# A state-space block between two feed-forward parts: the output projection of 29 phases in seven products of quarters

## The chip, the cores and the metric

The kernel runs on one core of a Trainium2 chip. The metric is the time of one execution in device microseconds, as the median of several runs. TensorE multiplies matrices into PSUM, VectorE (DVE) and ScalarE (ACT) work on PSUM and SBUF, GpSimd (POOL) on SBUF, and SyncE (SP) issues the transfers. Each engine takes its instructions in order.

## The reference

The input is 2 sequences of 512 tokens with 512 features, all in float32. The network adds four parts to it one after the other, each behind a layer norm: a block-sparse linear layer, a gated feed-forward part with quantised weights (512 to 1792 to 512), a state-space part with 128 heads of 64, and the same feed-forward part again. The state-space part, which the change is about, is this:

```python
proj = hidden_states @ in_proj_w.T                 # gate (8192), x (8192), B and C (8 groups of 128 each), dt
hBC = silu(causal_conv4(x, B, C))                  # four taps along the tokens
dt = softplus(dt + dt_bias)
Y_diag = einsum(M, x*dt)                           # inside chunks of 128 tokens
Y_off  = einsum(C, states) * state_decay           # from the chunks before
y = Y_diag + Y_off + D*x
y = y * rsqrt(mean(y*y) + EPS) * norm_w
y = y * silu(gate)
return y @ out_proj_w.T                            # 8192 -> 512
```

## The kernel before

The inner width 8192 is cut into 64 tiles of 128 features. A phase handles two tiles (`PP = 2`); there are 32 phases. A unit is one tile of one sequence, so a phase has four units (j, b). The loop over phases is a pipeline: in phase `ph` the front makes the x and gate projections of tiles 2ph and 2ph+1, the back runs the scan of phase ph-1, and the output projection is that of phase ph-2.

The x and gate projections already use seven products of quarters instead of eight (`seven`, L169): the weights' and the normed input's quarters are combined by additions (`left_sides` on GpSimd, `two_quarters` and others on the input), and seven products of two 128x128 by 128x512 matmuls each go into three PSUM accumulators. VectorE and ScalarE take partial sums out of them between the products. `seven` is a generator: each `next` puts one product with its additions into the queues.

The rest of a phase:

- `x_tokens` (L798): four transposes of a unit on TensorE, the multiply by dt on VectorE (`x_dt`), the decay on GpSimd (`x_dec`).
- `states` (L820): three matmuls into `pst`, then on VectorE one copy (L833) and four steps of 128x64 (L836).
- `scores` (L857): on ScalarE four activations, an exponential of `m` and one of `ce`; on VectorE, when `flush` is called, the multiply `m*gm` (L874); on GpSimd the multiply of `ce` (L880).
- `scan` (L888): the matmuls of a unit into one PSUM bank `py`; afterwards `gated` (L910) on VectorE takes it out (L912) and multiplies the gate into it in place (L913). The result, `gts[j, b]`, is 128 features by 512 tokens.
- `conv` (L706): ScalarE starts the convolution (L708), three further taps on VectorE (L711) are queued and put out by `drain`.
- `squares` (L918): a square on ScalarE and a sum on GpSimd (L920).
- `out_project` (L922): for each of the eight tiles of 128 tokens two matmuls 128x128 by 128x512 into one PSUM bank `po`, and one addition on VectorE into `acc` (L939). `acc` is the tile `x_sb`, 128 x 8 x 512.

PSUM has eight banks: three with the tag `proj`, three with `yo`, two with `tr`. In the phases from 2 on, the eight output products stand behind the first two scans, with `flush`, the scores and two to three taps between them, and the last two scans and the gate product follow:

```python
for k in range(4):
    between(2 * k)          # outs(2k)
    flush()
    if last or k:
        back_scores(4 + k)
    if last:
        drain(1 if k < 3 else 0)
```

The order of TensorE, VectorE and ScalarE is that of the program (`tc.manual_schedule`). GpSimd's and SP's queues are ordered by a planner. Every fourth phase also makes the B and C projections of the next group of eight tiles (`new_group`), seven products more.

Of the kernel before, what the change touches and what calls it, by code (L numbers as in the profile page):

```python
# [14 lines left out]
P = 128  # L15
# [22 lines left out]
def kernel(  # L38
# [42 lines left out]
    def weights():  # L81
        return keep.tile([P, KC, 2, P], F32, tag="w", name="w", bufs=3)
# [75 lines left out]
    def left_sides(w):  # L158

        a11, a12, a21, a22 = w[:, :KH, 0], w[:, KH:, 0], w[:, :KH, 1], w[:, KH:, 1]  # L160
        sq = keep.tile([P, 3, KH, P], F32, tag="ws", name="ws", bufs=3)
        s1, s2, s4 = sq[:, 0], sq[:, 1], sq[:, 2]
        nc.gpsimd.tensor_add(s1, a21, a22)  # L163
        nc.gpsimd.tensor_sub(a21, a11, a21)
        nc.gpsimd.tensor_sub(s2, s1, a11)
        nc.gpsimd.tensor_sub(s4, a12, s2)
        return a11, a12, a21, a22, s1, s2, s4

    def seven(left, tag, tmp, done, in_place):  # L169
# [16 lines left out]
        x, y, z = [psum.tile([P, SEQ], F32, tag=tag, name=f"{tag}{i}", bufs=3) for i in range(3)]  # L186
# [3 lines left out]
        yield  # L190
        product(y, s2, t2, True, False)
# [43 lines left out]
    def dequant_in(s, w, z, sc, scratch):  # L235

        cols = slice(s * SLAB, (s + 1) * SLAB)
        q = weights()
# [30 lines left out]
    def dequant_gate(s, scratch):  # L269
        return dequant_in(s, gate_w, gate_z, gate_s, scratch)  # L270

    def dequant_up(s, scratch):
        return dequant_in(s, up_w, up_z, up_s, scratch)
# [109 lines left out]
    def ffn(which, first, waiting, after, within):  # L383
# [3 lines left out]
        with tc.tile_pool(name=f"ffn{which}", bufs=1) as pool:  # L387
# [19 lines left out]
            def sg_tile(j, b):  # L407
                return pool.tile([P, SEQ], F32, tag=f"sg{j}{b}", name="sg")

# [44 lines left out]
            for b in range(2):  # L454
# [20 lines left out]
                if b == 0:  # L475
                    gq_next = left_sides(now(dequant_gate(1, scratch)))
                    quarters()
            last_quarter()
            uq_next = left_sides(now(dequant_up(1, scratch)))
            dequant_down(0)  # L480
            gq, uq = gq_next, uq_next
            for s in range(1, NSLAB):
# [18 lines left out]
                if more:  # L501
                    gq = left_sides(now(dequant_gate(s + 1, scratch)))
# [7 lines left out]
                if more:  # L510
                    uq = left_sides(now(dequant_up(s + 1, scratch)))
# [65 lines left out]
    def load_pair(*cts):  # L577

        w = weights()
# [11 lines left out]
        return left_sides(w)  # L591
# [9 lines left out]
    def step_weights():  # L601
        w_dt = weights()[:, :, 0, :]
# [43 lines left out]
    def mixer(waiting, step_args, loaded):  # L646

        with ExitStack() as st:
# [93 lines left out]
            def group_scores(made, shared, bs=range(2)):  # L742
                for b in bs:
                    b_t, c_t = made[b]
                    b_tok = grp.tile([P, NCH - 1, P], F32, tag=f"b_tok{b}", name="b_tok")
# [26 lines left out]
            def load_sums(ct, b):  # L772

                h0 = 2 * ct
                bc = wrk.tile([P, 2, SEQ], F32, name="bc", bufs=3)
# [12 lines left out]
            def g_front(left, gts):  # L788

                for j, b in units:  # L790
# [3 lines left out]
                    left, "proj", lambda j, b: gts[j, b], lambda j, b, ps: later.append((gts[j, b], ps)), False  # L794
# [25 lines left out]
            def states(ct, b, x_dec, b_tok):  # L820
# [12 lines left out]
                nc.vector.tensor_copy(state[:, 0], pst[:, 0])  # L833
# [54 lines left out]
            def scan(ct, b, xc, gt, x_dt, state, heads, tag):  # L888

                py = psum.tile([P, SEQ], F32, tag=tag, name="py", bufs=3)  # L890
# [54 lines left out]

            xcs, gts = {}, {}
# [14 lines left out]
            wg = load_pair(0, 1)  # L961
# [80 lines left out]
            for ph in range(1, n_ph + 1):  # L1042
# [39 lines left out]
                if last:  # L1082
                    wo = load_out(ph - 2)
                if not front:
# [4 lines left out]
                final = ph == n_ph - 1  # L1089
                if final:  # L1090
# [10 lines left out]
                next(steps)  # L1101
                if not last:
                    group_scores(made, groups[0], [0])
                else:
                    flush()
                next(steps)
                if not last:
                    group_scores(made, groups[0], [1])
                    made = None
                    flush()  # L1110
                else:
                    back_scores(2)
                tokens(2)
                tokens(3)
                next(steps)
                if last:
                    back_scores(3)
                next(steps)
                flush()
                if not last:  # L1120
                    back_scores(4)
                both_states(0)
                next(steps)
                drain(3)
                next(steps)
                run(steps)
                if not last:
                    drain(3)
                if last:
                    both_states(1)  # L1130
                scans = half_scan(units[:2])
                if not last:
                    drain()
                    both_states(1)
                    gate, later = g_front(wg, gts_new)
                else:
                    finish(scans)
                    scans = []

                def between(k):  # L1140
                    if last:
                        outs(k)
                    else:
                        next(gate, None)

                for k in range(4):
                    between(2 * k)
                    flush()
                    if last or k:
                        back_scores(4 + k)  # L1150
                    if last:
                        drain(1 if k < 3 else 0)
                    if made and k in (1, 2):
                        group_scores(made, groups[c0 // CTG], [k - 1])
                    between(2 * k + 1)
                    if k == 0:
                        finish(scans[:1])
                    elif k == 1:
                        finish(scans[1:])
                        scans.clear()  # L1160
                    if last:
                        drain(1 if k < 3 else 0)
                flush()
                all_squares()
                drain()
                made = None
                if new_group:


                    steps, made = group((c0 + PP) // CTG, wbc, "yo")  # L1170
                    for i, _ in enumerate(steps):
                        if i in (3, 5):
                            drain(3)
                if ph + 1 < n_ph:
                    wx = load_pair(NCT + c0 + PP, NCT + c0 + PP + 1)
                if last:
                    gate, later = g_front(wg, gts_new)
                if final:
                    up_q = weights()
                    ups = [dequant_half(up_q, 0, 0, up_w, up_z, up_s, old_tmp)]  # L1180
                finish(half_scan(units[2:], "proj" if new_group else "yo"))
                if last:
                    next(gate)
                else:
                    for u in units:
                        silu(xcs_new[u], xcs_new[u])
                half_scores(0, c0, heads_new)
                if last:
                    next(gate)
                if final:  # L1190
                    for f in gates:
                        f()
                    ups.append(dequant_half(up_q, 1, 0, up_w, up_z, up_s, old_group))
                drain(3)
                half_scores(1, c0, heads_new)
                if last:
                    next(gate)
# [225 lines left out]
```

## Time and profile before

| | us |
|---|---|
| median of 3 runs | 2285.58 (2284.93 to 2286.6) |
| the profiled execution | 2286.75 |
| its span | 2285.0 |
| TensorE busy | 2266.0 (99%) |
| VectorE busy | 1669.7 (73%) |
| ScalarE busy | 1162.5 (51%) |
| GpSimd busy | 1014.9 (44%) |
| output projection, L927, 992 matmul records | 436.8 |
| its additions, L939, 248 | 167.9 |

The busy time of an engine is that of its instructions in the profiled execution; matmul records overlap, so their sum is more than the time they occupy. The granted clock of TensorE was 0.999. A plain phase takes 49.0 us, one with a new group 61.0 and the one behind it 51.45.

### The profile page before, as it was taken

The numbers are of one execution on the slowest core, as the hardware profiler recorded it, in microseconds if no ns is written. First come the engines' busy times: TensorE is split into PE (matmuls) and PEld (weight loads), VectorE is DVE, ScalarE is ACT, GpSimd is POOL, SyncE is SP. The second block draws the span as 40 slices with busy tenths as digits, with TensorE's granted clock in tenths as the row PEclk, the third lists the DMA queues.
The fourth block names the chain that finished last, engine by engine and source line by source line (L and its number), as shares of the span: only waits on it lengthen the run. The fifth ranks groups of instructions, "written<-read, shape, count | busy, mean of one in ns | idle before, by whom it ended". The sixth has DMA issues, their size and how long they took to land.

```text
span 2285.0 us, 28307 instructions
## 1 busy us (share of the span) xinstructions
PE 2266.0 (99%) x10008; PEld 1273.9 (56%) x10008; DVE 1669.7 (73%) x2926; ACT 1162.5 (51%) x2474; POOL 1014.9 (44%) x971
## 2 busy tenths in 40 slices
PE   9999999999999999999999999999999999999999
PEld 5445865555555555555555555555555555544468
DVE  5456568787788787877877887888878778865553
ACT  4111056756665665666566556656565665631100
POOL 3765024545544444444445444444444454526620
PEclk9999999999999999999999999999999999999999
DMA  5663022222222222222122222221222321326600
GB/s 190 190 201 107 24 82 71 74 71 68 75 74 74 66 82 74 65 74 83 65 74 74 75 70 69 79 78 56 84 74 65 106 71 65 111 84 230 205 16 28
DMA packets 145773, 201.46 MB, mean 88 GB/s; under 512 B 7136, under 2 KB 92000, under 8 KB 145632
## 3 DMA queue, kind: packets, MB, share of 16 engines
q1 hardware_dynamic: 145056, 198.61, 27.0%
q8 instruction: 79, 1.29, 0.2%
q10 hardware_dynamic: 576, 1.05, 0.1%
q14 instruction: 62, 0.51, 0.1%
HBM read 194.91 MB, written 4.72 MB: 87 GB/s over the span
## 4 chain that ended last, share of the span: by engine, by line
PE 96%; DVE 2%; ACT 1%; DMA 1%; issue 0%; POOL 0%; ACTq 0%; SPq 0%; POOLq 0%; DVEq 0%
PE proj L177 39%; PE po L927 19%; PE yo L177 10%; PE ffn_o L533 7%; PE py L893 5%; PE pst L825 4%; PE py L902 3%; PE x_tr L804 2%; PE pg L463 1%; PE pu L463 1%; PE bs_o L323 1%; PE pgm L755 1%; PE ln_tr L134 0%; DMA bias_b<-in_bias_dram 0%; DVE xc L711 0%
## 5 line engine op out<-in xcount | busy, mean ns | idle before, releaser
L880 POOL TENSOR_TENSOR ce<-ce,c_t 128x384 f32<-128x384 f32 x256 | 267.4, 1049 | 450.9 <-ACT ce L876 445.1
L927 PE MATMUL po<-wo,gt 128*128 128x512 f32 x992 | 436.8, 595 | 0.0
L177 PE MATMUL proj<-xn_t,w 128*128 128x512 f32 x912 | 424.8, 596 | 3.3 <-DVE gt L192 1.7
L866 ACT ACTIVATE m<-bc,acs 128x128 f32<-128x128 f32 x1024 | 324.5, 389 | 4.4 <-PE py L893 4.4
L927 PEld LDWEIGHTS po<-wo,gt 128*128 128x128 f32 x992 | 184.6, 190 | 219.6 <-issue 194.4
L177 PE MATMUL proj<-tq,ws 128*128 128x512 f32 x608 | 278.5, 592 | 1.3 <-ACT gt L726 1.3
L177 PEld LDWEIGHTS proj<-xn_t,w 128*128 128x128 f32 x912 | 165.6, 190 | 182.6 <-issue 170.2
L874 DVE TENSOR_TENSOR m<-m,gm 128x512 f32<-128x512 f32 x256 | 219.2, 876 | 0.4 <-ACT m L873 0.4
L163 POOL TENSOR_TENSOR ws<-w 128x256 f32<-128x256 f32 x96 | 72.2, 752 | 323.3 <-DMA w<-in_win_t_dram 319.7
L711 DVE SCALAR_TENSOR_TENSOR xc<-proj,cw,xc 128x511 f32<-128x511 f32 (+2 forms) x288 | 213.3, 741 | 2.5
L812 POOL TENSOR_TENSOR x_dec<-x_dt,dec 128x384 f32<-128x384 f32 x128 | 131.6, 1038 | 130.8 <-DVE x_dt L808 122.3
L177 PEld LDWEIGHTS proj<-tq,ws 128*128 128x128 f32 x608 | 112.9, 190 | 131.2 <-issue 123.2
L920 POOL TENSOR_TENSOR sq_acc<-sq_acc,y 128x512 f32<-128x512 f32 x128 | 175.4, 1384 | 19.3 <-ACT y L919 19.2
L939 DVE TENSOR_TENSOR x_sb<-x_sb,po 128x512 f32<-128x512 f32 x248 | 167.9, 677 | 21.9 <-PE po L927 20.5
L893 PE MATMUL py<-m,x_dt 128*64 128x128 f32 x2048 | 180.9, 276 | 0.1
L873 ACT ACTIVATE m<-m 128x512 f32<-128x512 f32 x256 | 161.3, 630 | 7.4
L708 ACT ACTIVATE xc<-proj,cb,cw 128x512 f32<-128x512 f32 x96 | 71.2, 775 | 164.3 <-DVE proj L206 146.3
L902 PE MATMUL py<-ce,state 128*64 128x128 f32 x1536 | 149.5, 273 | 0.0
L177 PE MATMUL proj<-xn_t,ws 128*128 128x512 f32 x304 | 142.8, 592 | 0.0
L177 PE MATMUL proj<-tq,w 128*128 128x512 f32 x304 | 142.8, 592 | 0.0
L893 PEld LDWEIGHTS py<-m,x_dt 128*64 128x64 f32 x2048 | 122.1, 137 | 29.7 <-issue 20.5
L189 ACT COPY gt<-proj 128x512 f32<-128x512 f32 x32 | 18.7, 585 | 228.6 <-PE proj L177 228.5
(202 smaller groups left out, 3707.1 us busy)
## 6 DMA issues: line engine op xcount, KB each, us to landing
bc<-acs_d SPq DMA_DIRECT2D x128, 512.0 KB, 3.7
w<-in_win_t_dram SPq DMA_DIRECT2D x64, 512.0 KB, 3.8
wo<-in_wo_t_dram SPq DMA_DIRECT2D x31, 512.0 KB, 3.3
wi<-in_down_w_dram SPq DMA_DIRECT2D x14, 512.0 KB, 3.5
zi<-in_down_z_dram SPq DMA_DIRECT2D x14, 512.0 KB, 4.4
sf<-in_down_s_dram SPq DMA_DIRECT2D x14, 512.0 KB, 3.9
wi<-in_gate_w_dram SPq DMA_DIRECT2D x13, 512.0 KB, 4.1
zi<-in_gate_z_dram SPq DMA_DIRECT2D x13, 512.0 KB, 5.2
```

Of the source, the lines that this page charges most:

```text
L177: nc.tensor.matmul(ps, lhsT=a[:, kc, :], rhs=b[:, kc, :], start=(start and kc == 0), stop=(stop and kc == KH - 1), skip_group_check=True,)
L533: nc.tensor.matmul(ps, lhsT=a[:, k, :], rhs=b(k), start=(start and k == 0), stop=(stop and k == KF - 1), skip_group_check=True,)
L711: nc.vector.scalar_tensor_tensor(dst[:, s:], ps[:, : SEQ - s], cw[:, t, 3 - s : 4 - s], dst[:, s:], ALU.mult, ALU.add)
L866: nc.scalar.activation(m[:, c, :], bc[:, hh, c * P : (c + 1) * P], AF.Relu, bias=acs[:, t, h : h + 1], scale=-1.0,)
L873: nc.scalar.activation(m, m, AF.Exp, scale=-1.0)
L874: mults.append(lambda: nc.vector.tensor_mul(m, m, shared[b][2]))
L880: nc.gpsimd.tensor_mul(ce, ce, c_t[:, P:].rearrange("p (c l) -> p c l", l=P))
L893: nc.tensor.matmul(py[hh * HD : (hh + 1) * HD, c * P : (c + 1) * P], lhsT=x_dt[:, c, hh, :], rhs=m[:, c, :], start=True, stop=(c == 0),)
L902: nc.tensor.matmul(py[hh * HD : (hh + 1) * HD, c * P : (c + 1) * P], lhsT=state[:, c - 1, hh, :], rhs=ce[:, c - 1, :], start=False, stop=True,
L920: nc.gpsimd.tensor_add(sq_acc[:, b, :], sq_acc[:, b, :], y)
L927: nc.tensor.matmul(po, lhsT=gts[j, b][:, c * P : (c + 1) * P], rhs=wo[:, j, :], start=(j == 0), stop=(j == PP - 1),)
L939: nc.vector.tensor_add(acc[:, t, :], acc[:, t, :], po)
```

## The change

For the output projection of phases 0 to 28 (29 of 32) a phase's product, 1024 tokens by 256 features by 512 outputs, is cut into quarters: two sequences, two feature tiles, two halves of 256 outputs. Seven products of quarters replace eight. GpSimd makes three sums of the activations and changes one quarter in place (`out_left`), and does the same with the output weights (`out_right`).

Each product of a quarter is put out in two rounds (`r`) of two 128-token tiles: two matmuls 128x128 by 128x256 into one PSUM bank. So a phase has 14 such steps, each of two matmuls and one addition of 2x256 columns on VectorE. Three banks accumulate (x, y, z), and VectorE adds them, while they accumulate further, to the four quarters of `acc` and to a fifth accumulator, `common`, which takes the weights' third buffer. After phase 28's projection `merge` adds `common` to three quarters. The first round of seven steps stands between the steps of the x projection, the second behind the first two scans.

Other edits: the state's first copy moves from VectorE to ScalarE; the last two scans use the `tr` banks; the taps of the last two x results are put out in the gate product, or in the group's; in phases without a new group the gate product uses one `proj` and two `yo` banks; `bc` has two buffers instead of three, `b_tok` one instead of two; `w` and `ws` have two and a third under a tag of its own.

```diff
-        x, y, z = [psum.tile([P, SEQ], F32, tag=tag, name=f"{tag}{i}", bufs=3) for i in range(3)]
+        tags = [tag] * 3 if isinstance(tag, str) else tag
+        def bank(i):
+            return psum.tile([P, SEQ], F32, tag=tags[i], name=f"{tags[i]}{i}", bufs=3)
+        x = bank(0)
...
         yield
+        y, z = bank(1), bank(2)
...
-                bc = wrk.tile([P, 2, SEQ], F32, name="bc", bufs=3)
+                bc = wrk.tile([P, 2, SEQ], F32, name="bc", bufs=2)
...
-                nc.vector.tensor_copy(state[:, 0], pst[:, 0])
+                nc.scalar.copy(state[:, 0], pst[:, 0])
...
-                py = psum.tile([P, SEQ], F32, tag=tag, name="py", bufs=3)
+                py = psum.tile([P, SEQ], F32, tag=tag, name="py", bufs=2 if tag == "tr" else 3)
...
+            def out_right(wo):
+                b11, b12, b21, b22 = wo[:, 0, :DH], wo[:, 0, DH:], wo[:, 1, :DH], wo[:, 1, DH:]
+                t = sides(True).rearrange("p i k c -> p i (k c)")
+                nc.gpsimd.tensor_sub(t[:, 0], b12, b11)
+                nc.gpsimd.tensor_sub(t[:, 1], b22, t[:, 0])
+                nc.gpsimd.tensor_sub(b12, b22, b12)
+                nc.gpsimd.tensor_sub(t[:, 2], b21, t[:, 1])
+                return b11, t[:, 0], b21, b22, t[:, 1], b12, t[:, 2]
+            def out_left(gts):
+                a11, a12, a21, a22 = gts[0, 0], gts[1, 0], gts[0, 1], gts[1, 1]
+                s = sc.tile([P, 3, SEQ], F32, tag="sums", name="sums")
+                nc.gpsimd.tensor_add(s[:, 0], a21, a22)
+                nc.gpsimd.tensor_sub(a21, a11, a21)
+                nc.gpsimd.tensor_sub(s[:, 1], s[:, 0], a11)
+                nc.gpsimd.tensor_sub(s[:, 2], a12, s[:, 1])
+                return a11, a12, s[:, 0], s[:, 1], a21, s[:, 2], a22
+            def out_seven(left, right, fresh):
...
+                def product(r, k, start, stop, a, b):
+                    if start:
+                        banks[k] = psum.tile([P, 2, DH], F32, tag="yo", name="po7", bufs=3)
+                    for c in range(2):
+                        t = slice((2 * r + c) * P, (2 * r + c + 1) * P)
+                        nc.tensor.matmul(
+                            banks[k][:, c, :],
+                            lhsT=a[:, t],
+                            rhs=b,
+                            start=(start and c == 0),
+                            stop=stop,
+                            skip_group_check=True,
+                        )
+                def summed(r, k, q, new):
+                    q = q[:, 2 * r : 2 * r + 2]
+                    if fresh and new:
+                        nc.vector.tensor_copy(q, banks[k])
+                    else:
+                        nc.vector.tensor_add(q, q, banks[k])
...
+                    for k, start, stop, a, b, q, new in (
+                        ("x", True, False, a11, b11, common[0], True),
+                        ("y", True, False, s2, t2, q12, True),
+                        ("z", True, False, s1, t1, q22, True),
+                        ("x", False, True, a12, b21, q11, True),
+                        ("y", False, False, s3, t3, q22, False),
+                        ("z", False, True, s4, b22, q12, False),
+                        ("y", False, True, a22, t4, q21, True),
+                    ):
...
+            def merge():
+                for rows, cols in quarter[1:]:
+                    nc.gpsimd.tensor_add(acc[:, rows, cols], acc[:, rows, cols], common[0])
...
+                if mid:                      # phases 2 to 30
+                    outs7 = out_seven(lefts, rights, ph == 2)
+                    def o():
+                        product, summed = outs7.pop(0)
+                        product()
+                        summed()
+                    next(steps); o()
+                    next(steps); o()
+                    back_scores(2); tokens(2); tokens(3)
+                    o()
+                    next(steps); back_scores(3); o()
+                    next(steps); o()
+                    flush(); both_states(0)
+                    next(steps); back_scores(4); o()
+                    drain(3)
+                    next(steps); drain(3); o()
+                    run(steps)
+                    both_states(1)
+                    scans = half_scan(units[:2])
+                    finish(scans[:1]); o()
+                    finish(scans[1:]); o()
+                    flush(); back_scores(5); o(); o()
+                    flush(); back_scores(6)
+                    if made:
+                        group_scores(made, groups[c0 // CTG], [0])
+                    o(); o()
+                    flush(); back_scores(7)
+                    if made:
+                        group_scores(made, groups[c0 // CTG], [1])
+                    o()
+                    all_squares()
...
+                    if new_group:
+                        flush()
+                        steps, made = group((c0 + PP) // CTG, wbc, "yo")
+                        for i, _ in enumerate(steps):
+                            if i in (0, 1, 3, 5):
+                                drain(3)
+                        gate, later = g_front(wg, gts_new)
+                    else:
+                        gate, later = g_front(wg, gts_new, ("proj", "yo", "yo"))
+                        next(gate); flush()
+                    wx = load_pair(NCT + c0 + PP, NCT + c0 + PP + 1)
+                    wo = load_out(ph - 1)
+                    finish(half_scan(units[2:], "tr"))
+                    if ph < n_ph - 2:
+                        lefts, rights = out_left(gts), out_right(wo)
+                    if new_group:
+                        next(gate)
+                    half_scores(0, c0, heads_new); next(gate)
+                    drain(3)
+                    half_scores(1, c0, heads_new); next(gate)
+                    if not new_group:
+                        drain(3)
...
+                    next(gate)
+                    if new_group:
+                        drain(3)
+                    flush(); run(gate)
```

Calls that stand on lines of their own in the program are joined here with semicolons.

## The prediction

> **What bounds the kernel now.** I read the page first: engines, then the chain of waits, then the groups. TensorE is busy for all but 19 us of the span and owns the chain, so a matmul that goes away is time, as long as nothing else becomes late.
>
> ```profile
> PE 2266.0 (99%) x10008; PEld 1273.9 (56%) x10008; DVE 1669.7 (73%) x2926; ACT 1162.5 (51%) x2474; POOL 1014.9 (44%) x971
> PE 96%; DVE 2%; ACT 1%; DMA 1%; issue 0%; POOL 0%; ACTq 0%; SPq 0%; POOLq 0%; DVEq 0%
> ```
>
> Then the chain in order of time, which cuts one phase of the mixer (811.84 to 860.84, 49.0 us) into its stretches, and shows a stretch of 256-wide products in the first feed-forward part.
>
> ```profile
> 220.05 39.28 PE ffn_o L533 x182
> 811.84 12.21 PE proj L177 x28
> 824.92 3.44 PE proj L177 x8
> 829.23 3.44 PE proj L177 x8
> 834.01 5.15 PE proj L177 x12
> 843.71 13.93 PE po L927 x32
> ```
>
> A float32 matmul is two records here (L927: 992 records in 31 phases of 16 matmuls). So a 512-wide record takes 13.93 / 32 = 0.435 us in the output projection, 12.02 / 28 = 0.429 in the x and gate products, and a 256-wide one 39.28 / 182 = 0.216.
>
> Last the windows of the two halves of that phase, and VectorE's timeline in it. The columns of the windows are busy us with the count for PE, PEld, DVE, ACT, POOL.
>
> ```profile
> 811.84:836.00 24.16, 24.16 (x78) 12.34 (x79) 14.14 (x21) 19.02 (x40) 12.46 (x14) 1.00 0.21 65
> 836.00:860.84 24.84, 24.84 (x165) 14.77 (x163) 24.39 (x51) 11.88 (x29) 10.89 (x11) 1.00 0.26 87
> ```
>
> ```profile
> 832.71 0.69 DVE L197 TENSOR_TENSOR tmp<-tmp,proj 128x512 f32<-128x512 f32 x1 [2.35 <-PE proj L177]
> ```
>
> The reader should see that the share "DVE 73%" hides a stretch in which VectorE is busy for 24.39 of 24.84 us. It keeps up there only because each result of the output projection (two 512-wide matmuls, 1.74 us) asks for one addition.
>
> ```profile
> 834.03 2.09 DVE L874 TENSOR_TENSOR m<-m,gm 128x512 f32<-128x512 f32 x2
> 836.05 0.28 DVE L833 COPY state<-pst 128x128 f32<-128x128 f32 x1
> 836.36 0.86 DVE L836 SCALAR_TENSOR_TENSOR state<-state,e_last,pst 128x64 f32<-128x64 f32 x4
> 838.22 2.31 DVE L711 SCALAR_TENSOR_TENSOR xc<-tmp,cw,xc 128x511 f32<-128x511 f32 x3
> 840.46 0.69 DVE L206 TENSOR_TENSOR proj<-tmp,proj 128x512 f32<-128x512 f32 x1
> 841.05 0.69 DVE L211 TENSOR_TENSOR proj<-tmp,proj 128x512 f32<-128x512 f32 x1
> 843.84 0.74 DVE L912 SCALAR_TENSOR_TENSOR y<-xc,dsk,py 128x512 f32<-128x512 f32 x1
> 844.62 0.75 DVE L913 SCALAR_TENSOR_TENSOR gt<-y,nw,gt 128x512 f32<-128x512 f32 x1
> 846.73 0.68 DVE L939 TENSOR_TENSOR x_sb<-x_sb,po 128x512 f32<-128x512 f32 x1
> ```
>
> From start to start VectorE spends 0.60 on an addition that reads PSUM, 0.72 where the next needs its result, 2.24 on three taps, 0.77 on a unit's four state steps, 0.78 and 0.67 on L912 and L913. The multiply L874 takes 0.61 with GpSimd idle (820.27: two in 1.28) and 1.02 with it busy (834.03); its mean is 0.876.
>
> **The change, part by part.** I number the products of a changed phase X1..X7 (x), O1..O14 (output: two rounds of seven), G1..G7 (gate).
>
> TensorE. 16 matmuls, 13.93 us, become 28 of 256: 56 x 0.2158 = 12.08. Saved 1.85 a phase, 29 phases: -53.7 us. The weights load in 190 ns, below 216, as they do in L533.
>
> VectorE. The eight additions become fourteen of the same 512 elements, +3.6 us a phase; four copies (L833, 0.31 each) go to ScalarE. In sum VectorE still fits (38.5 busy of 49.0, then about 41.5 of 47.2), so the place decides. I walk its queue, as the built program orders it, from the end of X4, t = 0, where it is idle and waiting (the row at 832.71). O5 add, two L874, states, O6 add, three taps, X6 add, three taps, O7 add, X7 add: 1.32 + 0.60 + 1.22 + 1.54 + 0.60 + 2.24 + 0.60 + 2.24 + 0.60 + 0.60 = 11.56, with L874 at its 0.61. The first 1.32 are the two adds of X4. Now the moved copy: ScalarE has it behind the convolution start of X7 (L708, 0.74), which waits for VectorE's X7 add to end (0.69). A 128x128 copy on ScalarE is not in the trace; L866 of that size has 0.39. VectorE goes on 0.69 + 0.03 + 0.74 + 0.39 + 0.02 = 1.87 after it began the X7 add instead of 0.60: 1.27 idle. A copy of 0.28, as on VectorE, would make it 1.16. Then the states of two units, 1.54, and L912 of the first unit, 0.75: with 0.03 from TensorE to VectorE at the start it ends at 15.1.
>
> TensorE in the same time: O5 0.86, states 1.33, X5 1.72, O6 0.86, X6 1.72, O7 0.86, X7 1.72, states 1.33, two scans 3.22, O8 0.86 = 14.48. O9 takes the PSUM bank of the first scan, free only after that L912: it waits 0.65. O10 takes the second's bank: L913 0.67, O8 add 0.60, L912 0.75 end 2.05 after the first L912; TensorE is there at 0.96: 1.1 more. O14 accumulates on O12's result after VectorE has added it: L913, O9, L874, O10, O11, L874, O12 add end 6.4 after the first L912, TensorE is there at 5.6: 0.9 more with 0.1 for the handover. Stall 2.7 with every L874 at 0.61. Four of them lie on this path; the two of the early part stand beside GpSimd's x_dec exactly as the row at 834.03 does. At 1.02 each the stall is 4.3; I take the mean, 0.876: 3.8.
>
> What is late next: the six taps of X6 and X7 now stand in the gate stretch. After the third scan (end P): two units' L912 and L913 until P + 3.1, G2 add from P + 3.55, taps until P + 8.6, G4's first add ends at P + 9.3; G6 needs it and could start at P + 8.67: 0.7. Phases that bring a new group have seven more products between and four taps fewer there, so they lack this.
>
> The sum by kind: 15 plain phases, 3.8 + 0.7 - 1.85 = +2.66 each, +39.9. Seven with a new group, 3.8 - 1.85, +13.7. Seven behind those, where the group scores (2.44 of TensorE) cover O14's wait: 0.65 + 0.53 + 1.1 + 0.7 - 1.85 = +1.1 each, +7.9. Together +61.5. With L874 at 0.61 the three kinds give +1.55, +0.85 and +0.6, in all +33; at 1.02 +3.15, +2.45 and +1.4, in all +74.
>
> GpSimd gets four 512-wide and four 256-wide operations a phase: 4 x 1.27 (L920 alone) + 4 x 0.73 (L163) = 8.0, on 23.4 busy of 49.0. They are due at O2, 4.3 us into the next phase; the four of the activations stand behind the ce of the next heads and end about 3 us after that phase's nominal start. I cost them at nothing; each us later would be 29 us. The load of wo (3.3 us to landing) now waits for O14, stands on SP's queue ahead of one sums load (3.7) and has the 15 us of G and scans as cover. The x weights wait for X7 (4.0 from issue to their sides in this trace), then four sides (2.9) stand ahead of three ce on GpSimd; the last ends near 33.5 against the fourth scan at 35, without stalls. Two sums buffers instead of three: each load still has one whole unit's time, over 6 us. The merge is three GpSimd additions of 128x1024 once, 2.4 each by L231, behind the last round and some 30 us before its sums are read: between 0 and 7 us in all, taken as 0. The weight tags hold the same three buffers.
>
> A rule against the change is in the Trainium skill, GPSIMD Engine Reference, section Key points: GpSimd shares its SBUF interfaces with VectorE and collides with VectorE instructions that have two SBUF inputs. L874 shows it (0.61 against 1.02). L913 has two SBUF inputs as well, and shows 0.75 at 844.62 with a ce multiply of GpSimd starting inside it, and 0.75 with none. By the rule L913 would stretch like L874, and the one between L912 and O10 would add about 0.4 a phase, 12 us; I leave that out.
>
> The profiled execution took 2286.75 for a span of 2285.0, and the median of the runs is 2285.58. 2286.75 + 61.5 = 2348; less the 1.2 between execution and median, 2347. I forecast 2346.
>
> **The rivals.** (A) VectorE keeps pace and the matmuls' saving comes through. For it: VectorE's sum fits, and the first half of the phase has 10 us of idle (24.16 against 14.14) into which seven additions moved. Against it: O9, O10 and O14 hang on the second half. It decides at O12's add: the chain of 21.5 us before it must be over 2 us shorter than the rows make it, and the taps must not hold G6. In full -53.7: 2232; half, 2259. (B) The copy on ScalarE is not late, because the convolution start finds VectorE ahead: 29 x 1.27 = 37 less, 2309, or 2282 with L874 at 0.61. The row for ScalarE's order speaks against it, the unmeasured copy leaves room. (C) GpSimd becomes late as well, sums after O2 or every L874 beside it: one us a phase more, 2375.
>
> **How the numbers follow.** Forecast case (2318 to 2360 on its own) 0.56, A 0.22, B 0.13, C 0.09. About 0.2%, 4.6 us, is what a measurement of this kernel can tell from no change: B gives 0.05 of that, the rest of B is slower. Slower 0.56 + 0.08 + 0.09 = 0.73, the same 0.05, faster 0.22. The range reaches from 2268 (leaving out most of A and nothing of B, 0.16) to 2370 (leaving out the upper part of C, 0.04).
>
> **What would show it.** Right: plain phases of 51 to 52 us instead of 49.0; in TensorE's groups the output product with idle before it, released by VectorE's gating and additions, about 3 to 4 us a phase; VectorE idle for about 1.2 us before the second states, released by ScalarE. TensorE busy about 2212. Wrong: phases of 47.2, or TensorE waiting for GpSimd or a transfer.

## The result and the profile after

The changed kernel takes 2435.25 us (2431.08 to 2438.38) against 2285.99 for the kernel before in the same measurement: a ratio of 1.0652 [1.0632, 1.0672], 149.3 us slower. The profiled execution took 2438.4 for a span of 2436.7. The direction was as forecast; the forecast of 2346 and its range up to 2370 were not.

In the changed program the lines stand 23 further down: the multiply by the group scores is L897 (was L874), the gating L935 and L936 (L912, L913), the taps L734 (L711). L1014 is the new output product, L1028 its addition, L185 the x and gate products. From the page, engines and chain:

```profile
PE 2302.0 (94%) x10704; PEld 1436.7 (59%) x10704; DVE 1812.8 (74%) x2972; ACT 1192.8 (49%) x2602; POOL 1264.5 (52%) x1206
PE 62%; DVE 32%; ACT 2%; issue 2%; DMA 1%; POOL 1%; ACTq 0%; DVEq 0%; SPq 0%; POOLq 0%
```

VectorE's share of the chain went from 2% to 32%. TensorE's busy time rose, although it has less to do, and that is the first sign of something that the prediction did not have. The waits of TensorE (us in total, times, longest):

```profile
PE po L1014 <- DVE y L935: 82.7, 53, 2.8
PE yo L185 <- DVE gt L211: 19.7, 22, 1.3
PE po L1014 <- DVE x_sb L1028: 10.5, 18, 0.8
```

The places are those forecast: O9 and O10 wait for the gating (L935), O14 for an addition, G6 for the taps behind which L211 stands. TensorE's timeline of a plain phase, 816.12 to 869.35, shows O9, O10, O14 and G6:

```profile
844.93 1.94 PE L1014 MATMUL po<-ws,sums 128*128 128x256 f32 x4 [2.06 <-DVE y L935]
847.07 1.82 PE L1014 MATMUL po<-ws,sums 128*128 128x256 f32 x4 [0.19 <-DVE y L935]
851.75 1.13 PE L1014 MATMUL po<-ws,gt 128*128 128x256 f32 x4 [0.27 <-DVE x_sb L1028]
865.65 1.98 PE L185 MATMUL yo<-tq,w 128*128 128x512 f32 x4 [0.79 <-DVE gt L211]
```

O9 waits 2.06, not 0.65 to 1.18, and then O9 and O10 take 1.94 and 1.82 where four such records take 1.03 elsewhere. The windows tell why (the last columns are the granted clock, the DMA share and GB/s):

```profile
816.12:869.35 53.23, 49.92 (x266) 32.24 (x265) 44.10 (x72) 31.88 (x72) 32.01 (x32) 0.97 0.21 70
844.90:848.30 3.40, 3.17 (x7) 2.13 (x8) 3.35 (x6) 3.37 (x11) 2.48 (x2) 0.53 0.42 154
```

Right behind the gap the granted clock is half for 3.4 us. The trace's clock records hold 32 such stretches with 132.7 us in all, 28 of them in the 29 changed phases; the kernel before has 2 with 6.3 us.

VectorE's timeline in that phase is the queue that the prediction walked:

```profile
830.15 2.27 DVE L897 TENSOR_TENSOR m<-m,gm 128x512 f32<-128x512 f32 x2
834.48 3.10 DVE L734 SCALAR_TENSOR_TENSOR xc<-tmp,cw,xc 128x511 f32<-128x511 f32 x3
838.09 2.31 DVE L734 SCALAR_TENSOR_TENSOR xc<-proj,cw,xc 128x511 f32<-128x511 f32 x3
842.60 1.62 DVE L859 SCALAR_TENSOR_TENSOR state<-state,e_last,pst 128x64 f32<-128x64 f32 x8 [1.00 <-ACT state L856]
844.14 0.74 DVE L935 SCALAR_TENSOR_TENSOR y<-xc,dsk,py 128x512 f32<-128x512 f32 x1
```

and GpSimd beside it:

```profile
829.80 2.07 POOL L835 TENSOR_TENSOR x_dec<-x_dt,dec 128x384 f32<-128x384 f32 x2 [3.53 <-PE pst L848]
835.24 0.99 POOL L903 TENSOR_TENSOR ce<-ce,c_t 128x384 f32<-128x384 f32 x1 [3.37 <-ACT ce L899]
```

L935 ends 16.7 us after the end of X4 instead of 15.1. From start to start two rows make the difference: the pair of L897 took 2.19 (1.22 at the short price, 1.75 at the mean that was taken), and the first three taps 3.01 instead of 2.24. Both have GpSimd beside them. The three taps behind have it too, and took 2.22, the time of taps without it:

```profile
838.61 0.73 POOL L171 TENSOR_TENSOR ws<-w 128x256 f32<-128x256 f32 x1 [2.37 <-PE pst L848]
```

The difference is in the inputs: the first three read `tmp` and `xc`, both in SBUF, the three behind read `proj`, which is in PSUM, and `xc`. Over the whole trace, a tap of `tmp` took at most 0.75 with GpSimd idle (65 of them) and 1.10 to 1.54 where a GpSimd instruction ran when it started (27); none of the 288 taps of `proj` took over 0.75, though GpSimd ran at the start of 208. The copy on ScalarE left VectorE idle for 1.00, forecast 1.27.

By kind, from the start of a phase to the next (the phases before: plain 49.0, with a new group 61.0, behind a group 51.5, the first 42.3, the second 52.2):

| kernel | median us | ratio [95%] | plain | new group | behind a group | stretches at half clock |
|---|---|---|---|---|---|---|
| after | 2435.25 | 1.0652 [1.0632, 1.0672] | 54.4 | 65.3 | 56.5 | 32 |
| e1 gate product between | 2379.41 | 1.0406 [1.0390, 1.0421] | 52.7 | 63.3 | 53.9 | 2 |
| e2 multiplies early | 2359.79 | 1.0321 [1.0305, 1.0336] | 51.9 | 62.9 | 53.0 | 2 |
| e3 no additions | 2275.05 | 0.9951 [0.9937, 0.9965] | 48.4 | 59.4 | 51.0 | 3 |
| e4 no sums | 2425.88 | 1.0608 [1.0592, 1.0624] | 54.1 | 65.8 | 55.0 | 25 |
| e5 copy on VectorE | 2441.04 | 1.0660 [1.0639, 1.0682] | 54.7 | 65.6 | 57.4 | 30 |
| e6 three together | 2302.70 | 1.0069 [1.0054, 1.0085] | 49.7 | 60.5 | 52.0 | 2 |
| e7 taps first | 2312.02 | 1.0106 [1.0090, 1.0122] | 50.4 | 60.4 | 52.2 | 4 |
| e8 two multiplies on GpSimd | 2292.69 | 1.0024 [1.0014, 1.0033] | 49.5 | 61.3 | 50.2 | 3 |
| e9 filled gap | 2405.25 | 1.0510 [1.0494, 1.0525] | 53.5 | 64.5 | 54.5 | 2 |
| e10 addition first | 2299.94 | 1.0045 [1.0028, 1.0062] | 49.5 | 61.8 | 51.0 | 5 |
| e11 and taps early | 2288.12 | 0.9998 [0.9989, 1.0008] | 49.0 | 61.8 | 50.1 | 4 |
| e12 two places mended | 2274.87 | 0.9943 [0.9929, 0.9957] | 48.6 | 60.5 | 50.1 | 5 |

A plain phase here is the mean of 14, the last of which holds the merge. The stretches are those that begin between a kernel's first and last instruction.

### The profile page after: what moved, and what is told of

It is laid out like the page before. It is cut to its first block, busy times and chain, and to the rows that moved or that the text cites. A ratio compares the mean times of both kernels' runs of the same rounds, so it can differ in the third digit from the quotient of the medians.

```text
span 2436.7 us, 30234 instructions
## 1 busy us (share of the span) xinstructions
PE 2302.0 (94%) x10704; PEld 1436.7 (59%) x10704; DVE 1812.8 (74%) x2972; ACT 1192.8 (49%) x2602; POOL 1264.5 (52%) x1206
## 4 chain that ended last, share of the span: by engine, by line
PE 62%; DVE 32%; ACT 2%; issue 2%; DMA 1%; POOL 1%; ACTq 0%; DVEq 0%; SPq 0%; POOLq 0%
PE proj L185 21%; PE yo L185 13%; DVE xc L734 10%; PE po L1014 10%; PE ffn_o L556 7%; DVE state L859 4%; DVE m L897 4%; DVE y L935 3%; DVE x_sb L1028 3%; DVE gt L936 2%; PE x_tr L827 2%; PE py L916 2%; PE po L950 1%; PE py L925 1%; PE pg L486 1%
## 5 line engine op out<-in xcount | busy, mean ns | idle before, releaser
L903 POOL TENSOR_TENSOR ce<-ce,c_t 128x384 f32<-128x384 f32 x256 | 284.5, 1118 | 337.7 <-ACT ce L899 331.4
L185 PE MATMUL proj<-xn_t,w 128*128 128x512 f32 x824 | 385.4, 595 | 3.5 <-issue 2.5
L1028 DVE TENSOR_TENSOR x_sb<-x_sb,po 128x512 f32<-128x512 f32 x340 | 230.2, 681 | 78.7 <-PE po L1014 74.6
L185 PEld LDWEIGHTS proj<-xn_t,w 128*128 128x128 f32 x824 | 150.8, 190 | 146.5 <-issue 140.3
L1014 PE MATMUL po<-ws,sums 128*128 128x256 f32 x464 | 155.5, 467 | 84.8 <-DVE y L935 82.7
L897 DVE TENSOR_TENSOR m<-m,gm 128x512 f32<-128x512 f32 x256 | 234.8, 938 | 0.0
L734 DVE SCALAR_TENSOR_TENSOR xc<-proj,cw,xc 128x511 f32<-128x511 f32 (+2 forms) x288 | 212.8, 746 | 6.6
L185 PE MATMUL proj<-tq,ws 128*128 128x512 f32 x432 | 200.3, 595 | 0.0
L1014 PE MATMUL po<-wo,gt 128*128 128x256 f32 x696 | 197.2, 416 | 0.5 <-DVE x_sb L1026 0.5
L1014 PEld LDWEIGHTS po<-wo,gt 128*128 128x128 f32 x696 | 145.5, 213 | 66.6 <-issue 41.4
L1014 PEld LDWEIGHTS po<-ws,sums 128*128 128x128 f32 x464 | 97.7, 228 | 134.4 <-DVE y L935 72.0
L185 PE MATMUL yo<-tq,ws 128*128 128x512 f32 x336 | 153.4, 599 | 0.1
L185 PE MATMUL yo<-xn_t,w 128*128 128x512 f32 x328 | 151.2, 593 | 1.2 <-DVE gt L206 0.8
```

Source lines behind the costliest of these rows:

```text
L185: nc.tensor.matmul(ps, lhsT=a[:, kc, :], rhs=b[:, kc, :], start=(start and kc == 0), stop=(stop and kc == KH - 1), skip_group_check=True,)
L734: nc.vector.scalar_tensor_tensor(dst[:, s:], ps[:, : SEQ - s], cw[:, t, 3 - s : 4 - s], dst[:, s:], ALU.mult, ALU.add)
L897: mults.append(lambda: nc.vector.tensor_mul(m, m, shared[b][2]))
L903: nc.gpsimd.tensor_mul(ce, ce, c_t[:, P:].rearrange("p (c l) -> p c l", l=P))
L1014: nc.tensor.matmul(banks[k][:, c, :], lhsT=a[:, t], rhs=b, start=(start and c == 0), stop=stop, skip_group_check=True,)
L1028: nc.vector.tensor_add(q, q, banks[k])
```

## The experiments

**e3: are VectorE's additions the cost, and what does TensorE save?** The additions of the output products are left out from the third phase on.

```diff
                     if fresh and new:
                         nc.vector.tensor_copy(q, banks[k])
-                    else:
+                    elif fresh:
                         nc.vector.tensor_add(q, q, banks[k])
```

> Left out: the fourteen additions of the output products in phases 3 to 30, so the sums are wrong; all matmuls, transfers and GpSimd work stay. Theory 1 (the 256-wide products save their 53.7 us and the loss is VectorE's): no waits at O9 to O14, clock 1.00, plain phases of 47.2 to 48, the time 2233 to 2260. Rival (the 256-wide matmuls, the GpSimd sums or the fewer buffers cost time themselves): plain phases stay above 49.0 and the time above 2286.

Measured: 2275.05, 160 us less, above the range. The waits at O9, O10 and O14 are gone from these phases; G6's stays (18.3 us in 22 phases). Two more things kept it from the range. The first two phases are long (45.3 and 62.8). And TensorE saves less than was worked out: the phases with a new group, in which nothing waits any more, are 1.64 shorter, not 1.85. In a plain phase the second round shows where:

```profile
905.91 1.13 PE L1014 MATMUL po<-wo,gt 128*128 128x256 f32 x4
906.88 2.15 PE L1014 MATMUL po<-ws,sums 128*128 128x256 f32 x8
908.87 1.89 PE L1014 MATMUL po<-wo,gt 128*128 128x256 f32 x8
...
912.32 1.02 PE L185 MATMUL yo<-xn_t,w 128*128 128x512 f32 x2
```

From 905.91 to 912.32 are 6.41 us for 28 records, 0.229 each; O9 and O10 take 1.99 for eight. In the first round, between x products, a product of four takes 0.86. So a plain phase saves 13.93 - 6.41 - 7 x 0.86 = 1.5. Why the records take 0.229 there is not shown.

**e9: the clock by itself.** The products of O8 are issued three times, so that TensorE has something to do in the gap; no other queue changes.

```diff
                     finish(scans[:1])
+                    outs7[0][0]()
+                    outs7[0][0]()
                     o()
                     finish(scans[1:])
```

> The changed kernel, with the matmuls of O8 issued three times in place of once (the bank is started afresh each time, so the sum is the same): 4 x 2 more records of 0.216, 1.73 us more of TensorE a phase, in the stretch where it waits 2.06 to 2.3 us for O9. No engine does anything else in another order. Theory (the clock): the half-speed windows, 32 now with 132.7 us, come from that gap alone; with 0.3 to 0.6 us of it left they go to 5 or fewer, the wait for O9 stays as an end (VectorE's queue sets it) and O10 to O12 run at full speed: 1.2 to 1.9 us a phase less, 2380 to 2400. Rival (VectorE alone): the half speed lies in the shade of VectorE's queue and costs nothing; the time stays within 2425 to 2440. A third: a clock that falls for another reason than the gap, with the windows still at some 30.

Measured: 2405.25. With four matmuls (eight records) more in each changed phase the kernel is 30 us faster, and 32 stretches at half clock became 2 (6.8 us). So the gap made the clock fall, and the fall cost about 30 of the 149 us, a little less than the 35 to 55 of the theory; the rival, that it lies wholly in the shade of VectorE's queue, falls. TensorE's timeline of a plain phase of e9:

```profile
886.07 3.51 PE L1014 MATMUL po<-wo,gt 128*128 128x256 f32 x12
889.42 1.03 PE L1014 MATMUL po<-ws,sums 128*128 128x256 f32 x4
891.30 1.13 PE L1014 MATMUL po<-ws,sums 128*128 128x256 f32 x4 [0.86 <-DVE y L935]
894.10 1.13 PE L1014 MATMUL po<-wo,sums 128*128 128x256 f32 x4
896.07 1.13 PE L1014 MATMUL po<-ws,gt 128*128 128x256 f32 x4 [0.84 <-DVE x_sb L1028]
```

At full clock, and with 0.86 for a product, O9 costs 3.35 - 0.86 = 2.5 from O8's first start to its own, O10 1.88 - 0.86 = 1.0, O14 1.97 - 0.86 = 1.1. This is what VectorE's queue takes without the clock.

**e1: other work for TensorE in the gap.** The first gate product goes between O8 and O9; its copy on ScalarE stays where it was.

```diff
...
                     finish(scans[:1])
                     o()
+                    gate, later = g_front(wg, gts_new, "proj" if new_group else ("proj", "yo", "yo"), True)
+                    next(gate)
                     finish(scans[1:])
...
```

The last argument, `True`, is new (`split`): with it the generator stops between the first product and its copy.

> The first gate product G1 (1.72 us, needs nothing of VectorE) is put between O8 and O9, where TensorE waits 2.05 us for the first scan's bank; its copy on ScalarE stays where it was. VectorE's queue is unchanged. Theory 1 (VectorE's queue alone sets the phase, the half-speed clock behind the gap lies under VectorE's time): the gap is filled but O14 and the last scan still wait for VectorE, a plain phase goes from 54.4 to 53 or 53.5, the time to 2390 to 2410. Theory 2 (the half-speed windows that follow the gap cost time of their own): the gap falls below 0.5 us, the granted clock stays at 1.00, and a plain phase goes to 51 or 52, the time to 2345 to 2370.

Measured: 2379.41, between the two ranges. The clock is whole again (2 stretches), and the wait at O9 is shorter, but the gate product no longer stands between O14 and the last two scans, and the fourth scan now waits for a multiply.

```profile
PE po L1020 <- DVE y L941: 39.6, 58, 1.0
PE py L922 <- DVE m L903: 17.4, 22, 2.1
```

(In kernels with this edit the lines stand six further down: L903 is the multiply, L909 GpSimd's ce, L941 and L942 the gating, L1020 the output product, L1034 its addition.)

**e2: take the pair of L897 off the path to O9.** The second unit's two multiplies are issued one at a time, behind X3 and O4, three and two products earlier.

```diff
                     o()
                     next(steps)
+                    flush()
                     back_scores(3)
                     o()
+                    flush()
                     next(steps)
                     o()
-                    flush()
                     both_states(0)
```

> The two multiplies m*gm of the second unit move from behind O5 to behind X3 and O4, into idle time of VectorE (1.84 and 1.03 us there). Nothing else changes. Theory 1 (VectorE's queue from X4 on sets the waits at O9, O10 and O14): the chain shortens by the 2.2 us that the pair takes there, the wait at O9 falls from 2.05 to under 0.3, the clock stays at 1.00, a plain phase goes from 54.4 to about 51, the time to 2335 to 2355. Rival (a late operand of GpSimd or ScalarE is what O9 and O10 wait for): the waits stay and the time is within 10 us of 2435.

Measured: 2359.79, 5 above the range and 75 less than the changed kernel, the largest single gain of an order that does all the work. The waits for L935 halve (82.7 to 43.4) and the clock stays whole, since no gap is long enough.

**e5: the moved copy.** The first state copy goes back to VectorE.

```diff
-                nc.scalar.copy(state[:, 0], pst[:, 0])
+                nc.vector.tensor_copy(state[:, 0], pst[:, 0])
```

> Only the state's first copy goes back from ScalarE to VectorE (4 a phase). Theory (VectorE's queue sets O9): the 1.00 us in which VectorE waits for ScalarE before the second states goes, but four copies of 0.31 stand in the same queue, so the chain to O9 changes by -1.0 + 1.24 = +0.2 and the time by -5 to +15: 2430 to 2450. Rival (the copy that came late on ScalarE is what put the kernel over its time): 1 us and more a phase is gained, 2405 or less.

Measured: 2441.04, as expected: what ScalarE's order costs, VectorE saves. One thing was not expected: the first phase is back at 42.3, while with the copy on ScalarE it is 45.7, with an idle 2.49 us of TensorE that the profile calls "issue". So the moved copy costs 3.4 us once; a half-clock stretch behind that gap (at 387.72, absent in e5) is a part of it, and why the gap arises is open.

**e4: GpSimd's sums.** They are made once and then reused.

> Left out: the eight GpSimd operations on activations and output weights in all phases but the first, so the products are of stale sums; GpSimd loses 8.0 us a phase. Theory 1: GpSimd is not late and its operations lie where VectorE has no two-operand SBUF reads on its critical stretch, so little happens: 2415 to 2440. Rival (the added GpSimd work is what stretches VectorE and makes the missing 90 us): VectorE's multiplies and gating get their short times, a plain phase loses 2 us or more, the time falls to 2380 or less.

Measured: 2425.88, inside the range: 8 operations a phase less on GpSimd (1264.5 to 1038.1 us busy) give 9 us. That GpSimd's new sums are late, or in the way, is not the cost. GpSimd's other work beside VectorE (`x_dec`, `ce`) stays in this run.

**e6: three orders together.** e1, e2, and the second states ahead of X7 in place of behind it, so that the copy on ScalarE is early. The third:

```diff
                     o()
+                    both_states(1)
                     run(steps)
-                    both_states(1)
```

> G1 between O8 and O9, the second unit's multiplies early, and the second states' matmuls before X7 instead of behind it, so that ScalarE's copies stand ahead of the convolution start of X7. By the queue: O9 and O10 no longer wait; O14 waits about 0.7, the fourth scan about 1.3 for the multiplies, G6 about 1.2, a plain phase of 50.0 to 50.8, the time 2310 to 2335. Were the waits independent of each other, the two gains already measured alone (56 and 76) would add up to 2303 and the states would take another 20 to 29 off.

Measured: 2302.70, 132.6 less than the changed kernel and better than the range. What is left of the waits:

```profile
PE yo L185 <- DVE gt L213: 17.0, 22, 1.3
PE po L1020 <- DVE x_sb L1034: 7.7, 22, 0.9
PE py L922 <- DVE m L903: 7.4, 12, 1.2
```

**e7: three of the gate stretch's six taps, those of X6, ahead of the third and fourth gating**, to free G6 (`drain(3)` put ahead of `finish(half_scan(units[2:], "tr"))` in phases without a new group).

> As the run before, and in phases without a new group the three taps of X6 stand before the gating of the last two scans instead of behind it. By the queue G6's wait of about 0.9 to 1.2 goes, and nothing new is late: 22 phases by 0.8 to 1.2, 18 to 26 us below the run before. Rival (VectorE is simply full from X4 to G6, and the wait only moves to the gating): within 8 us of it.

Measured: 2312.02, 9 slower than e6: a miss. G6's wait went and a longer one came at G4, which waits for the addition behind G2, and that now stands behind the taps:

```profile
PE yo L185 <- DVE gt L208: 26.1, 22, 3.2
```

**e8: less on VectorE there.** e7, with the fourth unit's two multiplies on GpSimd (`by_pool` is true for them in the changed phases).

```diff
-                mults.append(lambda: nc.vector.tensor_mul(m, m, shared[b][2]))
+                mults.append(lambda: (nc.gpsimd if by_pool else nc.vector).tensor_mul(m, m, shared[b][2]))
```

> As the run before, and the multiplies m*gm of the fourth unit (two of eight) go from VectorE to GpSimd, in the changed phases. If VectorE's work from X4 to the last scan is what is left, it loses 1.4 to 2.5 us there, plain phases come to 47.3 to 48.2 and the time to 2240 to 2270, below the kernel before. Rival (GpSimd at some 35 us of 48 now is late with these multiplies, or its reads stretch VectorE by as much): no gain, 2290 or more.

Measured: 2292.69, above the range. G4's wait shrank to 7.1, but O14's rose from 7.7 to 25.3. VectorE's timeline of e8 names the reason, a multiply that takes 1.54 and has O12's addition behind it (812.58):

```profile
811.12 1.54 DVE L903 TENSOR_TENSOR m<-m,gm 128x512 f32<-128x512 f32 x1
```

**e10 and e11: that multiply behind the addition**, without and with the taps of e7; the multiplies on GpSimd only without a new group.

```diff
                     o()
                     o()
-                    flush()
                     back_scores(6)
                     ...
                     o()
+                    flush()
                     o()
                     flush()
```

> The three changes of e6 (2302.7), and the two m*gm of the fourth unit on GpSimd in the phases without a new group, and in all phases the m*gm of the fifth score behind O12's addition in place of ahead of it; the taps of X7 stay behind the gating as in e6. Theory (VectorE's order sets each wait): O14's wait, 25.3 us in 22 phases of e8, goes, because O12's addition no longer has a stretched multiply (1.53) ahead of it; the multiplies on GpSimd take 1.2 to 2 us from VectorE ahead of the third and fourth gating, so G6's wait of 0.77 (17.0 in 22 phases in e6) goes or halves. Phases 48.2 to 48.8 / 60.0 to 60.5 / 49.8 to 50.2, in all 2262 to 2280: below the kernel before (2286). Rival (the places are full: a wait that goes from one product comes back at the next, as in e7): 2290 to 2300.

> The kernel of e10 with the taps of X7 ahead of the third and fourth gating, as in e7 and e8. Theory: G6's wait is then gone and G4's small (7.1 us in 15 phases of e8); phases 48.2 to 48.8 / 60.2 / 49 to 50, 2255 to 2275, 0 to 10 below e10. Rival: taps ahead of the gating make the G4 addition late, 5 to 15 above e10.

Measured: 2299.94, where the rival had been put, and 2288.12, 11.8 below it and above its range. O14's wait is gone in both; in e10 G6 still waits (17.4 us in 22 phases), so the two multiplies on GpSimd do not free it and the taps do. New in both: 9.6 us once, for a multiply on GpSimd that stands behind the merge, and 1.4 in each of the seven phases with a new group.

**e12: these two places mended.** The old order with a new group, and the merge issued behind the fourth scan's gating.

> The kernel of e11 (2288.1) with two places mended that its trace names. In the seven phases with a new group the m*gm of the fifth score goes back ahead of O12's addition, as in e6, where such a phase took 60.5 and not 61.7 (TensorE's wait of 1.4 for L208 in seven phases goes). And the three additions that merge the common sum, 7.5 us of GpSimd, move from ahead of the fourth unit's multiplies, where TensorE waited 9.6 us for m once, to behind the fourth scan's gating, where GpSimd is idle for 13.9 us. Theory (each wait is set by the order of one engine's queue): 7 x 1.2 + 9.6 = 18 us less, and up to 5 of half-speed clock behind the long gap: 2264 to 2272, below the kernel before (2286) by 0.6 to 1%. Rival (the cover is gone and other waits take their place): 2276 to 2290.

Measured: 2274.87, a ratio of 0.9943 [0.9929, 0.9957]: 12 us below the kernel before, 3 above the range. The phases with a new group are 60.5 again. The wait behind the merge fell to 5.0 only, since one of its three additions and the squares still stand ahead of that multiply. A plain phase is 48.2, and TensorE is busy in all but 0.37 of it:

```profile
776.40:824.60 48.20, 47.83 (x265) 31.36 (x264) 41.91 (x71) 32.06 (x73) 34.98 (x34) 1.00 0.23 77
```

## Why the prediction was right in direction and wrong in size

What held. The loss is VectorE's, and its order decides more than its sum: without its additions the kernel is faster than before (e3), the same work in another order gives back 133 of the 149 us (e6), and with two multiplies of most phases moved to GpSimd as well the kernel is faster than before with every addition in it (e12). O9, O10, O14 and G6 are the places that wait. O10 and O14 are near their terms (1.0 and 1.1 in e9, forecast 1.1 and 0.9 to 1.4), and G6 with 0.97 (21.3 us in 22 phases of e9) is near 0.7. Rival B is out: the copy is late, by 1.00, and e5 moves nothing. Rival C's late sums are out: e4 gives 9 us. Its other half, every L874 beside GpSimd, came in part: the mean of L897 is 0.938, that of L874 was 0.876. Rival A would have needed an order that this change doesn't have.

What failed. The phases add up to 149.2 us more than before; the forecast had +61.5, made of -53.7 and +115.2.

- TensorE's term: -53.7 was 29 x 1.85. In e3 it is 1.64 in seven phases and 1.5 in the others, about -44. Products that follow each other directly take 0.229 a record and not 0.216; the record of 0.216 came from a feed-forward part. Short by 10.
- The walk to O9, the step that failed most: 0.65, or 1.18 with the mean of L874, against 2.3 (O9 at 844.93, less O8's start at 841.75 and its 0.86). The two L874 were priced at their mean, though the prediction itself said that they stand beside x_dec "exactly as the row at 834.03 does", which had 1.02 each; here they took 1.10 each. And the three taps of `tmp` were priced at 2.24, without GpSimd; a ce now runs into them, 3.01. Together they add 1.2; the copy gave 0.2 back, and 0.1 is the start of a product behind a wait (1.13 where 1.03 is usual).
- The rule on two SBUF inputs (the Trainium skill, GPSIMD Engine Reference, section Key points) was, beyond L874, weighed for L913 alone and left out. Ahead of O10 that was right: L936 took 0.75 at 844.91, with a ce of GpSimd starting inside it. Behind the third scan it took 0.93 and 1.14. The largest part that the sum had no price for, 0.77, is in the three taps of `tmp`, which have two SBUF inputs as well and which the prediction did not look at. The trace also shows why the row of L913 at 844.62 was no guide: it matters which starts first. All 59 of L936 into which a GpSimd instruction starts took 0.75; the 59 that started while one ran took 0.75 to 2.08, 1.07 in the median.
- The clock was in no step: +30 (e9). The forecast's own O9 wait of 0.65 would not have asked for it; it follows from the walk's error.
- The first phase: +3.4, the moved copy (e5).

The price of a gap could have been read ahead of the run. The phases before have no gap of 2 us, but the trace of before shows one in the last output products, behind the phases, and half the clock from 2014.55 for 3.4 us:

```profile
2013.24 0.66 PE L134 MATMUL ln_tr<-ident,tmp 128*128 128x128 f32 x4 [2.22 <-ACT tmp L119]
```

With -44, +30 and +3.4 the waits are left with 149.2 + 44 - 30 - 3.4 = 160 us, 5.5 a phase where the sum had 4.0. In a plain phase of e9 the four waits give 2.5 + 1.0 + 1.1 + 1.0 = 5.6 and, less the 1.5 that TensorE saves as in e3, 4.1 of the 4.5 measured; 0.4 stays unassigned.

Of what would show it, TensorE's busy time (2212) was wrong on two counts: up to 66 us of the 2302 are work at half speed, and the saving is smaller. Phases of 51 to 52 were forecast and 54.4 came.

## What to carry to other kernels

When an operation moves, price every instruction that it lands beside, not only itself: take its duration from the row with the same neighbour on GpSimd, and look at each queue that becomes full for operations with two SBUF inputs. Seven products for eight is a small gain (1.5 us of 49) that asks for 14 results to be added instead of 8; here it paid only when the additions that TensorE waits for stood ahead of the long work in VectorE's queue, and one wait removed came back at another product three times (e1, e7, e8) before the whole was below the kernel before (e12). A wait of TensorE that reaches about 2 us is dearer than it looks, and filling it with useless matmuls is a quick test of that.

## What the runs showed of the hardware that was not expected

A gap of 2.05 us and more in TensorE was, in 28 of 29 changed phases, enough for half the clock over the next 3.4 us. Another plain phase shows it beginning at O10, not at O9:

```profile
952.59 1.13 PE L1014 MATMUL po<-ws,sums 128*128 128x256 f32 x4 [2.06 <-DVE y L935]
954.73 2.04 PE L1014 MATMUL po<-ws,sums 128*128 128x256 f32 x4 [1.00 <-DVE y L935]
```

The half-speed stretches of three phases in a row begin at 845.1, 899.7 and 954.3, 54.6 apart, which is 16 times 3.413, and the records last 3.413 or 6.827. So the clock seems to be set on a grid of 3.413 us, and each of these stretches follows a grid window with about 2 us of idle in it: 1.85 to 2.28 us in the 28 phases, while no window at full clock with 1.63 or less was followed by one. In the 29th the gap of 2.05 (before 1767.3) lies across two windows with 1.42 and 1.63 of idle, and the clock stays whole. Gaps of 0.8 to 0.9 (O10, O14 and most of G6 in e9) had no such effect. The Trainium skill, TensorE: Matmul & The Clock Gate, section What's actually happening, states a free-running window of 3413 ns, which the grid agrees with; its section Why this matters for your kernels advises against gaps over about 3 us, and here a gap of 2.05 was too long.

A VectorE multiply of 128x512 with two SBUF inputs took from 0.68 (GpSimd idle) to 1.78 us (852.21 in the changed kernel), and GpSimd's ce beside VectorE 1.28 to 1.47 instead of 1.00.
